# Two of the first group's second-matrix block products computed on two levels in an fp32 Strassen-Winograd kernel on one Trainium2 core

## The chip, the cores and the metric

The kernel runs on one core of one Trainium2 chip. A core has a matrix engine (PE, with its weight loads listed as PEld), a vector engine (DVE), an activation engine (ACT), a general engine (POOL) and a queue engine (SP). Each runs its own instructions strictly in the order in which the program gives them, and waits on semaphores for the others. Transfers are issued by SP, ACT or POOL and carried out by 16 shared DMA engines. The metric is the device time of one execution in microseconds; before the change the median of three runs is 780.52 us (779.9 to 781.32).

## The reference

For 64 batches of 64 channels by 1024 columns, each batch picks one of 16 small matrices; the mixed rows go through a layer of 64 experts of rank 16, of which each token uses its 16 best; the result is added to the input.

```
W   = cond_weights[condition]                    # 64 x (64 x 64)
y   = einsum('bct,bcd->bdt', x, W)               # 4096 tokens x 1024
s   = y @ Wr.T                                   # 64 scores per token
G   = softmax of the 16 largest scores, 0 elsewhere
h   = einsum('nd,krd->nkr', y, A)                # 4096 x (64*16)
out = x + 2 * einsum('nkr,kdr->nd', h * G, B)
```

The kernel multiplies x by A first (product h), mixes the 64 channels of each batch afterwards (the 64x64 matmuls called zp), multiplies by the gates on DVE (into tiles hb), and multiplies by B (product o). So there are two products of 4096 x 1024 by 1024 x 1024 in fp32.

## The kernel before, in words

**Groups and block products.** The 4096 tokens are worked in 8 groups of 512. In each group, h and o are each split into 2 x 2 blocks and computed by seven block products p1 to p7 (the Strassen-Winograd scheme) in place of eight. The operands of p3, p5, p6 and p7 are sums of blocks: on the token side the steps s1 to s4 of `left_sums`, on the matrix side `a_sums` and `b_sums`.

**One level or two.** A block product can be computed directly ("one level", `whole_parent`): for each of two halves of the tokens, 4 matmuls of 128x512, so 8 in all. Or it is split again by the same scheme ("two levels", `parent`): seven leaf products of two matmuls each, 128x256 for o and 128x272 for h. Two levels need four token-side sums per block product on DVE (`prepare`, tiles `l_t`, in the order t1, t2, t3, t4), three copies or adds out of PSUM per ACT and DVE (`copied`, `part`, `third`, `fourth`), and seven matrix-side leaves. Before the change group 0 is computed on one level (its matrices are still arriving and being summed), groups 1 to 7 on two.

**The matrix leaves.** While group 0 runs, DVE makes the leaves of every block of A and B (`leaf_steps`, into tiles of pool `bsum`, five buffers), and POOL stores each to DRAM (`o_p_p` and `h_p_p`, L414). A buffer of `bsum` is free again once its store has landed. Blocks p5, p6, p7 and p4 of B also have three raw quarters stored (`raw_leaves`, L440). From group 1 on, SP fetches leaves back (`fetch`, L461) into a ring of 13 buffers in the order of use; four leaves of h per block stay in SBUF. Five buffers (`bp0`) open when a set of early tiles is given up (`second_level`), eight more (`bp1`) when the whole memory of the first group is (`steady`).

**The order of the work.** Nothing is scheduled by a planner: the program is written out by hand. `run` emits one block product: first half of its matmuls, then what the product before it leaves to do (`done`), then work hung on it as hooks: "mid", the next product's `prepare`, "late", the second half, "end". The tables after L943 say which leaf steps, sums, loads and fetches hang on which product (`h + n` and `o + n` count from the first product of h and of o in group 0). Because every engine works in program order, a step hung early on DVE holds up all that stands behind it.

**Group 0's o.** Before, `FIRST["o"]` is p1, p7, p6, p2, p5, p4, p3. The results are piled up in PSUM banks x, w and y (`PILES`): p6 adds onto p1's bank, p5 onto p6's, p3 onto p5's, p4 onto p7's. At each stage of the pile DVE adds the bank, or a copy of it made by ACT, into one quarter of the output tiles `o`, which POOL loads (L762) and stores (L768).

**The last product.** o's p3 in group 7 has no product after it. Its parts are added straight into the output tiles (`finish`), and two 128-row halves are stored by SP and ACT (L670). Its leaf p4 is accumulated into bank w, which an add of DVE reads first.

Of the kernel before, what the change touches and what calls it, by code (L numbers as in the profile page):

```python
# [29 lines left out]
def kernel(  # L30
# [141 lines left out]
    def scores_t(st):  # L172

        g = st["g"]
        s = acc.tile([P, 2, HN], F32, tag="acc", name=f"st_{g}")
        for h in range(2):
            for c in range(2 * CH):
                e = slice((c % 2) * K, (c % 2 + 1) * K)
                nc.tensor.matmul(
                    s[e, h, :],  # L180
                    lhsT=wr_sb[:, c, :],
                    rhs=xq[g, c // CH, h][:, c % CH, :],
                    start=(h == 0 and c < 2),
                    stop=(c >= 2 * CH - 2),
                    skip_group_check=True,
                )
        st_sb = mp0.tile([P, 2, BANK], F32, tag="m", name=f"st_sb_{g}")[:, 0, :]
        nc.scalar.copy(st_sb, s.rearrange("p h n -> p (h n)"))
        st["st"] = st_sb

    def turn(st):

        g = st["g"]
        sp = acc.tile([P, TPG, K], F32, tag="acc", name=f"sp_{g}")
        for i in range(TPG):
            nc.tensor.matmul(
                sp[:, i, :], lhsT=st["st"][:, ts(i, P)], rhs=two_i, start=True, stop=True
            )
        zr = mp0.tile([P, 2, BANK], F32, tag="m", name=f"zr_{g}")[:, 0, : TPG * K]
        zr = zr.rearrange("p (i k) -> p i k", k=K)  # L200
        nc.scalar.copy(zr, sp)
        st["zr"] = zr
# [137 lines left out]
    def left_sums(l):  # L340
# [35 lines left out]
        "h": ("p1", "p2", "p5", "p6", "p7", "p4", "p3"),  # L376
        "o": ("p1", "p7", "p6", "p2", "p5", "p4", "p3"),
    }
# [12 lines left out]
    for j, (r, c) in {"p1": (0, 0), "p2": (1, 0), "p3": (1, 1)}.items():  # L391
        (q11, _), (q21, q22) = quads(b_t[r, c], HALF)
        leaf_d.update({("o", j, "p1"): q11, ("o", j, "p2"): q21, ("o", j, "p3"): q22})

    unused, to_store = list(hb.values()), []

    def leaf_steps(k, j, block, apart=None):
# [4 lines left out]
        def staged(name):  # L402
            if apart is not None and unused:
                t = unused.pop().rearrange("p c k -> p (c k)")
                return t[:, : 2 * WIDTH[k]].rearrange("p (c k) -> p c k", c=2)
            t = bsum.tile([P, 2 * (HALF + KC)], F32, tag="leaf", name=name)
            return t[:, : 2 * WIDTH[k]].rearrange("p (c k) -> p c k", c=2)
# [34 lines left out]

    parents, to_fetch, ring, stay, fetched = [], [], [], {}, [0]

    def order_of_use():
        for n in range(len(parents) + 1):
            for p in LEAVES:
                m = n - 1 if p in ("p3", "p4") else n
                if 0 <= m < len(parents):
                    par = parents[m]  # L450
                    if par["level"] == 2 and (par["kind"] == "o" or p not in STAY):
                        to_fetch.append((par["kind"], par["j"], p))

    def fetch():
        if to_fetch:
            key = to_fetch.pop(0)
            pool = pools["bp0" if fetched[0] % RING < RING0 else "bp1"]
            fetched[0] += 1
            t = pool.tile([P, 2 * (HALF + KC)], F32, tag="b", name="l{}_{}_{}".format(*key))
            t = t[:, : 2 * WIDTH[key[0]]].rearrange("p (c k) -> p c k", c=2)  # L460
            nc.sync.dma_start(t, leaf_d[key])  # L461
            ring.append((key, t))

    def weights(k, j, p):
        if (k, j, p) in stay:
            return stay[k, j, p]
        key, t = ring.pop(0)
        assert key == (k, j, p)
        return t

# [3 lines left out]
    def parent(kind, st, j, left, done):  # L474

        g = st["g"]
        par = {"kind": kind, "g": g, "j": j, "level": 2, "done": done}

        width = WIDTH[kind]

        def begin():
            name = f"m_{g}_{kind}_{j}"
            if kind == "h" and (g > 1 or j not in ("p1", "p2", "p4")):
                t = pools["zp"].tile([P, 2, 2 * (HALF + KC)], F32, tag="z", name=name)
            else:
                t = pools["mp"].tile([P, 2, 2 * (HALF + KC)], F32, tag="m", name=name)
# [18 lines left out]
        def mm(bank, p, first):  # L505
            w, v = weights(kind, j, p), par["leaf"][p]
            for c in range(2):
# [7 lines left out]
                )  # L515
            if (kind, j, p) not in stay:
                fetch()

        par.update(begin=begin, prepare=prepare, mm=mm)
        return par  # L520

    PILES = {
        "h": dict(p1="X", p2="Y", p5="W", p6="x", p7="x", p4="x", p3="w"),
        "o": dict(p1="X", p7="W", p6="x", p2="Y", p5="x", p4="w", p3="x"),
    }

    def whole_parent(kind, st, j, left, whole, piles, done, copied=None):
# [24 lines left out]
        def copy_out(s):  # L554
            if copied is None:
                return
            if s == 0:
                got["m"] = mp0.tile([P, 2, BANK], F32, tag="m", name=f"m_0_{kind}_{j}")
            nc.scalar.copy(got["m"][:, s, :], piles[n, s])
# [21 lines left out]
    def run(par, before, after, hooks):  # L581
# [34 lines left out]
        if two:  # L616
# [3 lines left out]
            par["copied"] = copied  # L620
            if after is None:
                o = sts[-1]["os"][0, 1][:, 0, :HALF]
                add(o, o, par["bank"]["y"])
                add(o, o, par["val"]["r1"])
            else:
                part(par, 0, 0, "y", "r1")
# [6 lines left out]
        if tail:  # L633
            third()
        if two:
            par["mm"](par["bank"]["x"], "p6", False)
# [9 lines left out]
        if after is None:  # L646
            before["done"](before["m"], before["v"])
            bank("w")
# [10 lines left out]
        for f in hooks["end"]:  # L659
            f()  # L660

    def finish(par, before, st):

        o, q, val = st["os"][0, 1], par["q"], par["val"]

# [3 lines left out]
        def out_tile(s, queue):  # L669
            queue.dma_start(out[ts(st["g"] * TPG + s, P), ts(1, BANK)], o[:, s, :])  # L670

        into(1, 0, val["a"])
        par["mm"](par["bank"]["w"], "p7", True)
        par["mm"](par["bank"]["x"], "p5", False)
        par["copied"]("b")
        into(1, 1, par["bank"]["w"])
        z = acc.tile([P, HALF], F32, tag="acc", name="last_z")
        par["mm"](z, "p3", True)
        par["mm"](par["bank"]["w"], "p4", False)
        into(0, 1, val["b"])  # L680
        into(0, 1, z)
        out_tile(0, nc.sync)
        into(1, 1, val["b"])
        into(1, 0, par["bank"]["w"])
        out_tile(1, nc.scalar)

# [88 lines left out]
    def o_whole(st, whole):  # L775

        piles = {}

        copied = {"p1": (0, 0), "p6": (1, 0), "p5": (1, 1)}
        piled = {"p7": ("w", 1, 1), "p2": ("y", 0, 0), "p4": ("w", 1, 0), "p3": ("x", 0, 1)}  # L780

        def done(j):
            def f(m):
                if j in copied:
                    i, k = copied[j]
                    add(st["os"][i, k], st["os"][i, k], m)
                else:
                    n, i, k = piled[j]
                    add_piled(st["os"][i, k], piles, n)
                if j in ("p2", "p5", "p4", "p3"):  # L790
                    store(st, i, k)

            return f

        return [
            whole_parent("o", st, j, lambda: st["h_ops"], whole, piles, done(j), copied.get(j))
            for j in FIRST["o"]
# [139 lines left out]

    def fetches(n):
        for _ in range(n):
            fetch()  # L940

# [38 lines left out]
    at(o + 1, "mid", gated, st, 0, 1)  # L980
    at(o + 2, "mid", sums, st, "h_sums", "s1")
    at(o + 3, "mid", sums, st, "h_sums", "s4")
    at(o + 3, "end", b_sums, 4)
    for k, lst, n in (
        (h + 2, b_steps, 4),
        (h + 3, b_steps, 2),
        (h + 4, b_steps, 6),
        (h + 5, a_steps, 4),
        (h + 6, a_steps, 5),
        (o, a_steps, 2),  # L990
        (o + 1, b_steps, 7),
        (o + 2, a_steps, 7),
        (o + 3, b_steps, 1),
        (o + 3, a_steps, 2),
        (o + 4, b_steps, 6),
        (o + 5, b_steps, 2),
    ):
        at(k, "end", steps_of, lst, n)
    at(h + 1, "mid", gather, 1)
    for k, (i, j) in enumerate(((0, 0), (1, 0), (0, 1), (1, 1))):  # L1000
        at(o + 1 + k, "mid", load_x, 1, i, j)
    for n, when, j in ((h + 5, "mid", "p5"), (h + 6, "mid", "p6"), (o, "mid", "p7"), (o + 4, "mid", "p4")):
        at(n, when, raw_leaves, j, br[j])
    at(o + 4, "end", second_level)
    at(o + 5, "mid", fetches, 3)
    at(o + 5, "end", fetches, 2)
    h = sts[1]["h"]
    at(h + 0, "mid", fetches, 4)
    at(h + 0, "end", fetches, 4)

# [37 lines left out]
    for st in sts:  # L1048
        g, h, o = st["g"], st["h"], st["o"]
        if not g:  # L1050
            at(h + 6, "mid", load_res, st, (0, 0), (1, 1), (1, 0))
            at(o + 5, "mid", load_res, st, (0, 1))
        else:
# [67 lines left out]
```

## Time and profile before

| What | Value |
|---|---|
| Median of three runs | 780.52 us (779.9 to 781.32) |
| The profiled execution's own time | 780.21 us |
| Its span (first to last event of the core) | 778.4 us |
| DVE busy | 623.8 us (80%) |
| ACT busy | 184.5 us (24%) |
| POOL busy | 73.8 us (9%) |
| Leaf matmul of o, 128x256 | 379 to 383 ns listed, pairs start 0.86 us apart |
| Leaf stores of o by POOL | 28 of 256 KB |

The span is what the core's records cover; the execution's own time has 1.8 us more around it. A line of the timeline gives the start, the duration, the engine, the source line, the operation, its tiles (out<-in, with buffer numbers left out), how often it is repeated, and in square brackets the idle time before it and what ended that. The chain of waits is followed back from the last instruction: each piece is released by the one before it. PE's durations are modelled at their ends, so distances between starts are the better measure of its pace. In the table of stretches the column PEclk is the clock granted to PE, 1.00 being full speed.

### The profile page before, as it was taken

The numbers are of one execution on the slowest core, as the hardware profiler recorded it, in microseconds if no ns is written. First come the engines' busy times: TensorE is split into PE (matmuls) and PEld (weight loads), VectorE is DVE, ScalarE is ACT, GpSimd is POOL, SyncE is SP. The second block draws the span as 40 slices with busy tenths as digits, with TensorE's granted clock in tenths as the row PEclk, the third lists the DMA queues.
The fourth block names the chain that finished last, engine by engine and source line by source line (L and its number), as shares of the span: only waits on it lengthen the run. The fifth ranks groups of instructions, "written<-read, shape, count | busy, mean of one in ns | idle before, by whom it ended". The sixth has DMA issues, their size and how long they took to land.

```text
span 778.4 us, 14669 instructions
## 1 busy us (share of the span) xinstructions
PE 770.6 (99%) x5348; PEld 610.9 (78%) x5348; DVE 623.8 (80%) x1310; ACT 184.5 (24%) x490; POOL 73.8 (9%) x103
## 2 busy tenths in 40 slices
PE   9999999999999999999999999999999999999997
PEld 4445448888888888887888888888888888888886
DVE  4789867678889878897788976889768888688987
ACT  1120002223122222222222222222222231222221
POOL 4235352000200020000200010000200000000000
PEclk9999999999999999999999999999999999999999
DMA  9959678656788768896788958799488893687997
GB/s 331 399 182 332 264 248 300 211 157 238 226 272 298 264 220 287 281 304 226 244 284 278 319 194 283 258 294 330 137 313 268 283 355 113 229 257 250 341 383 259
DMA packets 107607, 208.50 MB, mean 268 GB/s; under 512 B 11072, under 2 KB 27200, under 8 KB 106640
## 3 DMA queue, kind: packets, MB, share of 16 engines
q1 hardware_dynamic: 100496, 186.83, 70.6%
q0 software_dynamic: 6608, 19.95, 7.4%
q8 instruction: 43, 0.70, 0.4%
q10 hardware_dynamic: 432, 0.79, 0.3%
q14 instruction: 28, 0.23, 0.1%
HBM read 174.41 MB, written 33.11 MB: 267 GB/s over the span
## 4 chain that ended last, share of the span: by engine, by line
PE 95%; DVE 3%; DMA 1%; issue 0%; ACT 0%; ACTq 0%; DVEq 0%
PE h_p_x L508 23%; PE o_p_x L508 20%; PE h_p_w L508 12%; PE o_p_w L508 10%; PE h_p_y L508 6%; PE o_p_y L508 5%; PE zp L321 4%; PE o_x L545 4%; PE h_x L545 3%; PE h_w L545 2%; PE o_w L545 2%; DMA x<-in_x_t_dram 1%; DVE o L87 1%; PE sw L221 1%; PE gp L301 1%; PE h_y L545 1%
## 5 line engine op out<-in xcount | busy, mean ns | idle before, releaser
L508 PE MATMUL o_p_x<-lo_p_p,l_t 128*128 128x256 f32 x584 | 142.9, 379 | 0.0
L508 PEld LDWEIGHTS o_p_x<-lo_p_p,l_t 128*128 128x128 f32 x584 | 111.0, 190 | 15.4
L87 DVE TENSOR_TENSOR o<-o,m_o_p 128x1024 f32<-128x1024 f32 x65 | 78.0, 1219 | 0.6
L157 POOL DMA_INDIRECT w_st<-in_cw_dram,idx x32 | 34.9, 1089 | 429.1 <-PE zp L321 412.9
L87 DVE TENSOR_TENSOR m_h_p<-h_p_w,l_a 128x272 f32<-128x272 f32 x49 | 21.6, 440 | 62.6 <-PE h_p_w L508 60.3
L87 DVE TENSOR_TENSOR m_h_p<-m_h_p,m_h_p 128x1088 f32<-128x1088 f32 x49 | 62.3, 1284 | 0.2
L508 PE MATMUL h_p_x<-a,l_t 128*128 128x272 f32 x224 | 60.5, 392 | 0.0
L508 PE MATMUL h_p_w<-lh_p_p,l_t 128*128 128x272 f32 x196 | 53.8, 397 | 0.0
L508 PE MATMUL h_p_x<-lh_p_p,l_t 128*128 128x272 f32 x196 | 52.9, 392 | 0.0
L508 PE MATMUL o_p_w<-lo_p_p,l_t 128*128 128x256 f32 x196 | 51.1, 383 | 0.0
L508 PEld LDWEIGHTS h_p_x<-a,l_t 128*128 128x128 f32 x224 | 42.6, 190 | 8.6
L601 ACT COPY l_b<-h_p_x 128x272 f32<-128x272 f32 x49 | 18.9, 385 | 121.9 <-PE h_p_x L508 117.2
L334 DVE TENSOR_TENSOR hb<-zp,gg 128x512 f32<-128x512 f32 x64 | 39.9, 684 | 7.0 <-PE zp L321 7.0
L508 PE MATMUL h_p_x<-at,l_t 128*128 128x272 f32 x168 | 45.4, 392 | 0.0
L508 PEld LDWEIGHTS h_p_x<-lh_p_p,l_t 128*128 128x128 f32 x196 | 37.2, 190 | 7.5
L601 ACT COPY l_b<-o_p_x 128x256 f32<-128x256 f32 x49 | 18.2, 372 | 103.8 <-PE o_p_x L508 103.8
L508 PEld LDWEIGHTS h_p_w<-lh_p_p,l_t 128*128 128x128 f32 x196 | 36.5, 191 | 7.0
L508 PEld LDWEIGHTS o_p_w<-lo_p_p,l_t 128*128 128x128 f32 x196 | 36.6, 190 | 5.2
L87 DVE TENSOR_TENSOR m_o_p<-o_p_w,l_a 128x256 f32<-128x256 f32 x48 | 20.3, 423 | 22.5 <-PE o_p_w L508 22.5
L321 PEld LDWEIGHTS zp<-w_st,m_h_p 64*64 64x64 f32 x2048 | 31.7, 135 | 7.9 <-issue 7.7
L508 PEld LDWEIGHTS h_p_x<-at,l_t 128*128 128x128 f32 x168 | 31.9, 190 | 6.6
L608 ACT COPY m_h_p<-h_p_x 128x272 f32<-128x272 f32 x49 | 18.9, 385 | 70.7 <-PE h_p_x L508 70.7
(174 smaller groups left out, 1387.3 us busy)
## 6 DMA issues: line engine op xcount, KB each, us to landing
lo_p_p<-o_p_p SPq DMA_DIRECT2D x280, 256.0 KB, 3.7
lh_p_p<-h_p_p SPq DMA_DIRECT2D x147, 272.0 KB, 5.4
lo_p_p<-in_b_t_dram SPq DMA_DIRECT2D x63, 256.0 KB, 4.5
x<-in_x_t_dram SPq DMA_DIRECT2D x31, 512.0 KB, 5.4
o<-in_x_dram SPq DMA_DIRECT2D x28, 512.0 KB, 7.2
out_dram<-o SPq DMA_DIRECT2D x27, 512.0 KB, 5.7
o_p_p<-os_p_p POOLq DMA_DIRECT2D x28, 256.0 KB
b<-in_b_t_dram SPq DMA_DIRECT2D x4, 1024.0 KB, 17.9
```

Source lines behind the costliest of these rows:

```text
L87: nc.vector.tensor_tensor(o, a, b, ALU.add)
L157: nc.gpsimd.indirect_dma_start(out=w_st[:, i, :], out_offset=None, in_=cw, in_offset=bass.IndirectOffsetOnAxis(ap=idx[:, n : n + 1], axis=0),)
L221: nc.tensor.matmul(sw[r, i, ts(k, K // 2)].rearrange("p (d k) -> p d k", d=2), lhsT=ws[g][r, i, :], rhs=halves(st["z"][i // 2, k])[r, i % ...
L301: nc.tensor.transpose(gp[:, i, :], st["g2"][i].rearrange("p a k -> p (a k)"), ident)
L321: nc.tensor.matmul(zp[b][e * D : (e + 1) * D, c, s, :], lhsT=halves(z)[r, s, c // 2, ds(c % 2 * P + e * D, D)], rhs=ws[g][r, 2 * i + s, :] ...
L334: nc.vector.tensor_tensor(tokens(hb[j, i])[:, :, :, b, :], zp[b], g_ij[:, :, :, b, :], ALU.mult)
L508: nc.tensor.matmul(bank, lhsT=v[:, c, :], rhs=w[:, c, :width], start=first and c == 0, stop=c == 1, skip_group_check=True,)
L545: nc.tensor.matmul(piles[n, s], lhsT=left()[j][:, c, ts(s, P)], rhs=w, start=c == 0 and PILES[kind][j].isupper(), stop=c == CH - 1, skip_g ...
L601: nc.scalar.copy(par["val"][n], par["bank"]["x"])
L608: nc.scalar.copy(before["q"][0][1], before["bank"]["x"])
```

## The change

1. In group 0, o's p5 and p3 become two-level products. `FIRST["o"]` becomes p1, p7, p2, p6, p4, p5, p3, so these two are the last before group 1. Their leaves p1 and p2 are used where they lie in SBUF; the other five of each are fetched from DRAM through the ring.
2. p6's value, copied from PSUM, is now added into three quarters of the output one by one, p5's into two, p3's into one.
3. `second_level` and the first five fetches (all of `bp0`) move one product earlier, to o + 3 and o + 4; eight fetches for `bp1` stay at group 1's first product. A used buffer is refilled in its own pool.
4. The six leaves of A's first two blocks are staged in four `hb` tiles, one tile of `mp0` and one of `extra`, none in `bsum`.
5. The hooks of leaf steps, sums s1 and s4, `b_sums(4)` and the raw leaves of p4 move: among others `b_sums(4)` and seven A steps to o + 2, the four p6 steps of B and two A steps to o + 3, two B steps each to o + 5 and o + 6.
6. The last product's leaf p4 gets a bank of its own, p3 is accumulated on bank x, p2's output quarter is added in two halves, and the order of the last adds and stores changes.

```diff
-        "o": ("p1", "p7", "p6", "p2", "p5", "p4", "p3"),
+        "o": ("p1", "p7", "p2", "p6", "p4", "p5", "p3"),
...
+    unused.append(mp0.tile([P, CH, HN], F32, tag="m", name="place_m"))
+    unused.append(extra.tile([P, CH, HN], F32, tag="ex", name="place_ex"))
...
-            if apart is not None and unused:
+            if apart is not None:
...
+        here = STAY if kind == "h" else () if g else ("p1", "p2")
...
+        to_fetch[-2:] = to_fetch[:-3:-1]
+    def fetch(name):
         if to_fetch:
             key = to_fetch.pop(0)
-            pool = pools["bp0" if fetched[0] % RING < RING0 else "bp1"]
-            fetched[0] += 1
-            t = pool.tile([P, 2 * (HALF + KC)], F32, tag="b", name="l{}_{}_{}".format(*key))
+            t = pools[name].tile([P, 2 * (HALF + KC)], F32, tag="b", name="l{}_{}_{}".format(*key))
...
-        "o": dict(p1="X", p7="W", p6="x", p2="Y", p5="x", p4="w", p3="x"),
+        "o": dict(p1="X", p7="W", p2="Y", p6="x", p4="w"),
...
+    def begin_last(par, before, st):
+        o, p = st["os"][0, 0][:, 0, :], st["os"][0, 1][:, 0, :HALF]
+        add(o, o, before["m"][:, 0, :])
+        add(p, p, par["bank"]["y"])
+        add(p, p, par["val"]["r1"])
...
+        mm(w, "p7", True)
+        mm(x_, "p5", False)
+        par["copied"]("b")
+        z = acc.tile([P, HALF], F32, tag="acc", name="last_z")
+        mm(z, "p4", True)
+        mm(x_, "p3", False)
+        q = st["os"][0, 0]
+        add(q[:, 1, :], q[:, 1, :], before["m"][:, 1, :])
+        store(st, 0, 0)
         into(1, 0, val["a"])
-        par["mm"](par["bank"]["w"], "p7", True)
-        par["mm"](par["bank"]["x"], "p5", False)
-        par["copied"]("b")
-        into(1, 1, par["bank"]["w"])
-        z = acc.tile([P, HALF], F32, tag="acc", name="last_z")
-        par["mm"](z, "p3", True)
-        par["mm"](par["bank"]["w"], "p4", False)
...
+        into(1, 1, w)
+        into(1, 0, w)
+        into(1, 1, val["b"])
+        into(1, 0, z)
+        out_tile(1, nc.scalar)
+        into(0, 1, x_)
         out_tile(0, nc.sync)
...
+                elif j == "p6":
+                    kept["a"] = m
+                    into(1, 0, m)
+                    into(1, 1, m)
+                elif j == "p4":
+                    into(1, 0, pile="w", last=True)
+                    into(0, 1, kept["a"])
+                elif j == "p5":
+                    into(1, 1, m, last=True)
+                    into(0, 1, m)
...
-    at(o + 2, "mid", sums, st, "h_sums", "s1")
-    at(o + 3, "mid", sums, st, "h_sums", "s4")
-    at(o + 3, "end", b_sums, 4)
+    at(o + 3, "mid", sums, st, "h_sums", "s1")
+    at(o + 4, "mid", sums, st, "h_sums", "s4")
+    at(o + 2, "end", b_sums, 4)
...
-        (h + 3, b_steps, 2),
-        (h + 4, b_steps, 6),
+        (h + 3, b_steps, 4),
+        (h + 4, b_steps, 4),
...
-        (o + 1, b_steps, 7),
+        (o + 1, b_steps, 8),
         (o + 2, a_steps, 7),
-        (o + 3, b_steps, 1),
+        (o + 3, b_steps, 4),
         (o + 3, a_steps, 2),
-        (o + 4, b_steps, 6),
         (o + 5, b_steps, 2),
+        (o + 6, b_steps, 2),
...
-    at(o + 4, "end", second_level)
-    at(o + 5, "mid", fetches, 3)
-    at(o + 5, "end", fetches, 2)
+    at(o + 3, "end", second_level)
+    at(o + 4, "mid", fetches, RING0, "bp0")
```

## The prediction

> **What bounds the kernel now.** I read the page's busy shares and chain first, then the chain piece by piece, then the timeline of DVE and POOL while group 0's o runs, and last the end of the span.
>
> ```profile
> PE 770.6 (99%) x5348; PEld 610.9 (78%) x5348; DVE 623.8 (80%) x1310; ACT 184.5 (24%) x490; POOL 73.8 (9%) x103
> PE 95%; DVE 3%; DMA 1%; issue 0%; ACT 0%; ACTq 0%; DVEq 0%
> ```
>
> PE sets the time: 95% of the chain, and hardly 8 us of the span without a matmul. So a matmul saved is worth its whole duration, and a wait of PE costs its whole length, wherever it lies. The chain, group 0:
>
> ```profile
> 54.94 0.68 DVE m_h_p L87
> 55.62 0.04 issue
> 55.66 7.13 PE h_w L545 x16
> ...
> 80.40 6.87 PE o_x L545 x16
> 87.26 6.87 PE o_y L545 x16
> ...
> 114.73 0.92 PE h_p_x L508 x4
> ```
>
> Only one DVE piece stands here (0.72 us at 54.94); a one-level product takes 6.87 us, and PE then runs without a gap into group 1. Now DVE and POOL in the same stretch:
>
> ```profile
> 96.22 2.29 DVE L90 TENSOR_TENSOR b<-b,bt 128x2048 f32<-128x2048 f32 x1
> 98.42 0.68 DVE L90 TENSOR_TENSOR os_p_p<-b 128x512 f32<-128x512 f32 x1
> 99.02 0.72 DVE L90 TENSOR_TENSOR hs_p_p<-a 128x544 f32<-128x544 f32 x1
> 99.77 0.72 DVE L90 TENSOR_TENSOR hs_p_p<-a,hs_p_p 128x544 f32<-128x544 f32 x1
> 100.42 1.28 DVE L87 TENSOR_TENSOR o<-o,o_y 128x512 f32<-128x512 f32 x2
> 101.61 0.69 DVE L90 TENSOR_TENSOR os_p_p<-bt 128x512 f32<-128x512 f32 x1
> 101.99 0.71 POOL L768 DMA_DIRECT2D out_dram<-o  x1 [0.65 <-DVE o L87]
> 102.70 2.13 POOL L440 DMA_DIRECT2D o_p_p<-b  x3
> 104.44 3.05 POOL L414 DMA_DIRECT2D o_p_p<-os_p_p  x5
> 108.83 0.69 DVE L90 TENSOR_TENSOR os_p_p<-b,os_p_p 128x512 f32<-128x512 f32 x1 [3.88 <-DMA o_p_p<-os_p_p]
> 112.98 0.42 DVE L87 TENSOR_TENSOR l_t<-x 128x256 f32<-128x256 f32 x1
> 113.43 0.42 DVE L90 TENSOR_TENSOR l_t<-l_t,x 128x256 f32<-128x256 f32 x1
> ```
>
> Two things are to be seen. DVE adds bank y at 100.42, though PE finished it at 94.13: it runs six us behind PE. And it stands 3.88 us for a buffer whose leaf was made at 101.61 but whose store POOL could issue only at 104.44, behind an output store and three raw leaves. Both are free now, because one-level products need little from DVE; the first that PE needs is t2 of group 1 (ended 113.85, used near 116.5).
>
> **The change, part by part.** *Matmuls.* One level is 8 matmuls, 6.87 us. Two levels are seven leaves of 0.864 (o leaves run as 1.73 for two in the chain), 6.05 us. Two products: 2 x 0.82 = 1.64 us less on PE.
>
> *Staging.* All five `bsum` buffers are now free when the B steps begin at 31.99. In the profile the fourth step waited 5.60 us, until 39.73, for a store; now the sixth is the first to wait, for the same store. DVE does the score routing, six B steps in place of four, and `b_sums(1)` with this lead; the add before PE's h_w, at 54.93, comes at about 51.6. PE is ready at 54.94, so the 0.72 us piece goes: -0.7 us. The other moved hooks up to here are covered: PE's next needs (hb with s3, ended 71.92 for a use at 71.97 before) come earlier too. If the lead were lost, 0.7 us would stay.
>
> *The DVE queue ahead of p5.* This decides. Let E be the end of PE's p2, now third of the seven and two products ahead of p5: 80.40 + 6.87 - 0.72 = 86.5. `b_sums(4)` overwrites the matrix that p2 reads, so DVE cannot start it before E; by then it has the rest of its queue done (its wait at 81 to 84.6 for leaf stores shrinks, because stores are issued some 2 us earlier and five fetches of SP that landed around 78 to 84 have moved away; before, it would be through near 87.8, 1.3 after E). From E, in program order, with distances between starts in the trace:
>
> - `b_sums(4)` 2.20 (96.22 to 98.42); seven A steps 4.95 (the same seven ran 88.99 to 93.94); two adds of y 1.19; s1 1.13 (a 1024 add); four B steps 2.66 (101.61 to 104.27); one A step 0.75: E + 12.88.
> - the second A step, which needs a `bsum` buffer; the sixth one back is the first of those four B steps, so it waits for that store.
> - then 0.65, two adds of p6's copy, s4 (3 x 1.14), t1 0.45, t2 0.42: 4.94.
>
> PE meanwhile: p6 and p4 (2 x 6.87), then p5's leaves p1 and p2 (1.73), which read a tile made at s1: E + 15.47. The next leaf needs t2. Without a wait for the store DVE has t2 at E + 17.82: PE stands 2.35 us. The store: POOL must issue the output store when the y adds end (E + 8.34 + 0.29), then the three raw leaves, then this one, exactly the sequence shown above, where 6.84 us lie between the output store's issue (101.99) and DVE's release (108.83). There the queue was already 1.6 us behind with older stores, here by my sum about 1.0, so 6.2: release at E + 14.9, t2 at E + 19.8, **PE stands 4.4 us**. With the full 6.84 it is 4.9, and with DVE 1.3 late at E 6.2; below, 2.35. I take 4.4: the copied sequence is the nearest row. Behind the waiting A step stand all output adds, s4 and `prepare`; only PE waits for those.
>
> *After that.* DVE has t3, t4, one part, the w adds (1.19), one 1024 add, t1 and t2 of p3: about 4.3 us; PE has six leaves, 5.2. The 1024 add needs the fourth output tile, loaded by POOL after the late A step's store; about 1 us of slack. Each of `bp0`'s five buffers is refilled on use and needed 5.2 us later; o fetches in group 1 land in 3.7 us at the median, those of h in 5.4, and here POOL's stores run beside them. 0 to 1.5 us, I take 0 (o fetches are the nearer row). Group 1's first fetches wait on group 0's last output store, as before, with five us in hand.
>
> *Extra DVE and ACT work* of the two products (8 token sums of 0.42, 6 parts, 3 more 1024 adds) is inside the sums above; ACT's copies are hidden, it is 24% busy.
>
> *The clock.* [...]
>
> ```profile
> 773.60 1.13 PE L508 MATMUL o_p_w<-lo_p_p,sum_p 128*128 128x256 f32 x4 [0.93 <-DVE o L87]
> ...
> 774.77 0.42 DVE L87 TENSOR_TENSOR o<-o,o_p_w 128x256 f32<-128x256 f32 x1
> ```
> ```profile
> 776.00:776.20 0.20, 0.00 (x0) 0.00 (x0) 0.00 (x0) 0.00 (x0) 0.00 (x0) 1.00 0.56 205
> 776.20:776.40 0.20, 0.00 (x0) 0.00 (x0) 0.00 (x0) 0.00 (x0) 0.00 (x0) 0.58 1.02 389
> 776.40:776.60 0.20, 0.00 (x0) 0.00 (x0) 0.00 (x0) 0.00 (x0) 0.00 (x0) 0.50 1.02 389
> ```
>
> The row: the clock fell to half at 776.23, 1.5 us after the last matmul. [...] I take 1.5; no run here shows a gap of this length inside the work.
>
> *The end.* Leaf p4 no longer waits 0.93 us for DVE, so DVE bounds: after the add that ended at 770.17 come two adds of 512 (about 0.6 each), ten of 256 (0.34, with 0.1 to 0.2 more where one needs the last), against one 1024 and nine of 256 ending at 775.19 before. I get 774.8: -0.4 us (0 to -0.8).
>
> Sum: -1.64 - 0.7 - 0.4 + 4.4 + 1.5 = +3.1 us on the profiled 780.21, whose span is 778.4. That execution lies 0.3 below the median; I add to the median: **783.6 us**.
>
> **The rivals.** *The stall without the clock:* the same gap, full clock: 780.52 + 1.6 = 782.1, with the short stall 780.1. [...] *No stall, the other side:* if DVE reached t2 by E + 15.47, only the gains stay: 780.52 - 2.74 = 777.8. It needs 2.35 us less DVE work between `b_sums(4)` and t2 and no store wait; the gain passes into loss where the stall exceeds 2.7 us. Against it: each duration is a measured one of the same instruction, and DVE cannot pass its own queue.
>
> **How the numbers follow.** Stall with clock 0.47 (782.3 to 785.5), stall alone 0.21 (780.1 to 783.2), more late 0.18 (785 to 789), no stall 0.14 (777.3 to 779). Range 779.8 to 787.0: it leaves out nearly all of the last and a third of the third case, 2 in 10. About 0.2% is what a measurement can tell from no change: 779.0 to 782.1. Faster is the last case less a little, 0.13; within, half of the stall alone and some of its neighbours, 0.17; slower 0.70.
>
> **What would show it.** Right: a gap of 2 to 5 us on PE before the third leaf of group 0's o p5, its releaser an l_t subtraction of DVE; ahead of that DVE idle some 2 us before an A step, for a leaf store; the granted clock at half somewhere in the next 7 us; no 0.7 us gap before h_w; no 0.93 us wait in the last leaves; 24 more PE pieces (each fp32 matmul is listed as two, and two products go from 8 to 14). Wrong: PE going through p5 without a gap, because DVE was further ahead; or a gap elsewhere, at fetched leaves of p3 or group 1; or full clock after the gap.

## The result

The changed kernel takes 786.79 us at the median (785.49 to 787.75), the kernel before 780.62 us (779.9 to 781.53) beside it: a ratio of 1.0076, 95% interval 1.0063 to 1.0089. It is slower by 6.2 us. The prediction was 783.6 us: the right sign, half the loss, and a time inside the range, but only 0.2 us below its upper end of 787.0; two of the six executions lay above it. All later comparisons with the kernel before stand against its runs on the chips of the experiments, 780.83 to 780.84 us at the median.

### The profile page after: what moved, and what is told of

Same layout as the page of the kernel before. It is cut to its first block, busy times and chain, and to the rows that moved or that the text cites. A ratio compares the mean times of both kernels' runs of the same rounds, so it can differ in the third digit from the quotient of the medians.

```text
span 785.7 us, 14781 instructions
## 1 busy us (share of the span) xinstructions
PE 772.1 (98%) x5372; PEld 618.6 (79%) x5372; DVE 632.3 (80%) x1327; ACT 186.8 (24%) x496; POOL 74.7 (10%) x103
## 4 chain that ended last, share of the span: by engine, by line
PE 95%; DVE 2%; issue 1%; ACT 0%; POOL 0%; DVEq 0%; POOLq 0%
PE h_p_x L517 23%; PE o_p_x L517 21%; PE h_p_w L517 12%; PE o_p_w L517 11%; PE h_p_y L517 6%; PE o_p_y L517 5%; PE zp L322 4%; PE h_x L558 4%; PE o_w L558 2%; PE h_w L558 2%; PE o_x L558 2%; PE sw L222 1%; DVE o L87 1%; PE gp L302 1%; PE o_y L558 1%
## 5 line engine op out<-in xcount | busy, mean ns | idle before, releaser
L517 PE MATMUL o_p_x<-lo_p_p,l_t 128*128 128x256 f32 x612 | 151.8, 383 | 5.0 <-issue 5.0
L517 PEld LDWEIGHTS o_p_x<-lo_p_p,l_t 128*128 128x128 f32 x612 | 117.3, 192 | 21.9 <-issue 5.4
L87 DVE TENSOR_TENSOR o<-o,m_o_p 128x1024 f32<-128x1024 f32 (+1 forms) x70 | 82.8, 1203 | 0.5
L517 PE MATMUL o_p_w<-lo_p_p,l_t 128*128 128x256 f32 x204 | 54.1, 388 | 0.0
L517 PEld LDWEIGHTS o_p_w<-lo_p_p,l_t 128*128 128x128 f32 x204 | 38.7, 193 | 5.6
```

The source lines that it names most:

```text
L87: nc.vector.tensor_tensor(o, a, b, ALU.add)
L517: nc.tensor.matmul(bank, lhsT=v[:, c, :], rhs=w[:, c, :width], start=first and c == 0, stop=c == 1, skip_group_check=True,)
```

## The profile after

The profiled execution took 787.5 us, with a span of 785.7. Two rows of its page:

```profile
PE 772.1 (98%) x5372; PEld 618.6 (79%) x5372; DVE 632.3 (80%) x1327; ACT 186.8 (24%) x496; POOL 74.7 (10%) x103
PEclk9999989999999999999999999999999999999999
```

There are 24 PE pieces more, as worked out, and one slice of 40, the sixth (98 to 118 us), in which the granted clock is not full. The chain of waits through that stretch (start, duration, what):

```profile
51.62 3.63 PE h_x L558 x8
55.25 6.87 PE h_w L558 x16
...
79.72 6.87 PE o_y L558 x16
86.59 6.87 PE o_x L558 x16
...
101.19 0.86 PE o_p_y L517 x4
102.05 5.04 issue
107.08 2.05 PE o_p_x L517 x4
...
110.84 2.94 PE o_p_x L517 x8
...
118.96 0.92 PE h_p_x L517 x4
```

Three things are to be seen. The DVE piece ahead of h_w is gone. PE stands 5.04 us before the third leaf of group 0's o p5 (the chain calls it "issue", since the subtraction for t2, which the leaf reads, had ended 0.1 us before). And the leaves behind the gap are slow: the ten from 107.08 to 118.96 take 11.88 us where ten take 8.65 at full clock. DVE and POOL in the timeline of the same execution:

```profile
86.63 2.29 DVE L90 TENSOR_TENSOR b<-b,bt 128x2048 f32<-128x2048 f32 x1 [1.31 <-PE o_y L558]
...
95.35 0.72 POOL L789 DMA_DIRECT2D out_dram<-o  x1 [1.41 <-DVE o L87]
96.06 2.13 POOL L444 DMA_DIRECT2D o_p_p<-b  x3
...
97.80 2.53 POOL L418 DMA_DIRECT2D o_p_p<-os_p_p  x4
...
102.06 0.73 DVE L90 TENSOR_TENSOR hs_p_p<-a,hs_p_p 128x544 f32<-128x544 f32 x1 [2.57 <-DMA o_p_p<-os_p_p]
...
106.56 0.42 DVE L90 TENSOR_TENSOR l_t<-l_t,sum_p 128x256 f32<-128x256 f32 x1
```

This is the queue of the prediction, instruction by instruction. E, the end of PE's p2, is 86.59, and DVE had stood 1.31 us for it. The output store is issued at 95.35, three raw leaves behind it, then the leaf store that the second A step waits for; DVE is released at 102.06, 6.71 us after the output store's issue, and t2 ends at 106.98. The table of stretches shows the clock (columns: stretch, its length; busy time and count of PE, PEld, DVE, ACT, POOL; PEclk; DMA share; GB/s):

```profile
106.40:109.40 3.00, 2.31 (x6) 1.90 (x7) 2.97 (x8) 0.23 (x1) 0.00 (x0) 0.50 0.31 123
109.40:112.40 3.00, 3.00 (x9) 2.38 (x8) 2.35 (x5) 0.14 (x1) 0.73 (x1) 0.50 0.71 257
...
113.20:114.00 0.80, 0.80 (x5) 0.72 (x4) 0.80 (x2) 0.18 (x1) 0.00 (x0) 1.00 0.59 207
```

In the trace's record of the clock it is at half from 106.35 for 6.827 us, twice 3.413.

**The account.** I take the start of the same PE piece, counted from the end of the program, in both traces. At group 1's start PE is 5.96 us later than before: -0.68 when group 0's third o product begins (80.40 before, 79.72 after; PE ran 0.32 late from its start on, and the staging brought 1.0), -1.64 for the two products, +5.04 of gap, +3.23 of slow leaves. Of the span's 7.3 us the rest is +1.13 near 205 us, -0.67 between 300 and 400 and +1.22 at 741 (short stops of PE, below), and -0.36 at the end. The medians differ by 6.17; the changed kernel's profiled execution lies 0.7 above its median, that of the kernel before 0.3 below.

## The experiments

| Run | Median us | Ratio to before (95%) | PE's gap at p5's third leaf |
|---|---|---|---|
| changed kernel | 786.79 | 1.0076 (1.0063 to 1.0089) | 5.04 |
| e3_warm | 783.13 | 1.0032 (1.002 to 1.0044) | 0.58, ahead of it dummy work |
| e4_raw_later | 782.85 | 1.0029 (1.0018 to 1.004) | 2.51 |
| e2_one_step | 781.65 | 1.0008 (1.0002 to 1.0015) | 1.73 |
| e1_no_gap | 779.68 | 0.9985 (0.9979 to 0.9992) | none |
| e8_bp1_later | 779.86 | 0.9992 (0.9985 to 0.9998) | none |
| e7_shift | 779.63 | 0.9987 (0.998 to 0.9995) | none |
| e9_one_more_stays | 779.14 | 0.9977 (0.9967 to 0.9986) | none |
| e10_stays_shift | 778.24 | 0.9963 (0.995 to 0.9977) | none |
| e5_staging (from before) | 779.47 | 0.9983 (0.9977 to 0.999) | no such leaf |
| e6_tail (from before) | 781.17 | 1.0002 (0.9994 to 1.001) | no such leaf |

The first theory: all of the loss is DVE's queue between the end of p2 and t2, and what the clock makes of the gap. Its rivals: the loss lies in the fetched leaves, in the DMA engines, or in the other parts of the change.

### No gap

```diff
-        (o + 2, a_steps, 7),
-        (o + 3, b_steps, 4),
+        (o + 2, a_steps, 3),
+        (o + 3, b_steps, 2),
...
-        (o + 5, b_steps, 2),
-        (o + 6, b_steps, 2),
+        (o + 5, b_steps, 3),
+        (o + 6, b_steps, 3),
...
+    at(o, "mid", steps_of, a_steps, 2)
+    at(o + 2, "mid", steps_of, a_steps, 2)
```

> The changed kernel with hooks alone moved: of the seven A steps behind b_sums(4) at o + 2 four go earlier (two at o 'mid', two at o + 2 'mid'), and of the four B steps at o + 3 two go later (three each at o + 5 and o + 6). Theory (the loss is DVE's queue between the end of p2 and t2, and what the clock makes of it): from the end E of PE's p2, DVE needs 2.2 (b_sums) + 3 x 0.71 (A steps) + 1.2 (y adds) + 1.1 (s1) + 2.7 (four steps in the two hooks) + 4.4 (adds, s4, t1, t2) = 13.6 us, and PE asks for t2 at E + 15.5: no gap of PE before the third leaf of p5, full clock afterwards, and only the gains stay: 780.6 - 1.64 - 0.7 - 0.4 = 777.9 us (777.3 to 778.9), ratio to before 0.9965. Rival (what the changed kernel lost lies elsewhere too, in late fetches of p3 and of group 1 or in PE's later short stops): the gap goes but 780 to 783 us are left. Second rival (the steps moved earlier only move the wait forward, since the store queue of POOL is what is full): DVE waits for a buffer at o or at o + 2 'mid' and PE's gap stays at 2 us or more, 782 to 785 us.

Measured: 779.68 us. The chain of this kernel:

```profile
100.74 0.86 PE o_p_y L517 x4
101.60 0.86 PE o_p_x L517 x4
102.47 0.86 PE o_p_w L517 x4
...
108.54 5.98 DMA lo_p_p<-o_p_p
114.52 0.14 issue
114.66 1.10 PE o_p_w L517 x4
```

The gap is gone, the granted clock is 1.00 in every stretch from 96 to 122 us (its mean is 0.998 or more in all 21 executions), and the time falls by 7.1 us: DVE's queue and the clock did make the loss. Six hook lines, with all the rest of the change in place, turn it from 0.8% slower into 0.15% faster than before. The second rival falls. But 1.8 us of the expected gain are missing, and the first rival has a share in them: the last leaf of p3, issued by SP at 108.54 when its ring buffer came free, landed 5.98 us later, and PE waited 0.97 us more than between two leaves. In the changed kernel the same leaf had the same lead (issued at 117.27 for a use at 122.41) and was in time. Another 0.33 us lie outside the span: this kernel, like the four built on it (e7 to e10), has 2.1 us there, all others 1.8; why was not found. The rest are in the main short stops of PE, taken up below.

### One step

```diff
-        (o + 3, a_steps, 2),
+        (o + 3, a_steps, 1),
+        (o + 4, a_steps, 1),
```

> The changed kernel with one step moved: the second of the two A steps at o + 3, the one that waited 2.57 us for a bsum buffer, goes to o + 4, behind prepare of p5. Theory (the gap of 5.0 us is 2.6 of that wait and 2.4 of DVE's own work): DVE reaches t2 3.3 us earlier (2.57 wait and 0.73 step), the gap of PE is 1.7 us (1.3 to 2.2), too short for the clock to fall: 786.8 - 3.3 - 3.2 = 780.3 us (779.5 to 781). [...] Second rival (the loss is the amount of DVE work, the wait only filled time that would have been lost anyway): the gap stays above 3.5 us, 784 to 786.5.

Measured: 781.65 us, above the expected 780.3. The chain:

```profile
102.19 1.73 issue
103.93 1.10 PE o_p_x L517 x4
```

The gap is 1.73 us as expected: moving one step of 0.73 us took 3.31 us away, 2.57 of them the wait for its buffer. So the rival that takes the wait for mere filling falls. The clock stayed full, 1.00 from 102 to 110 us in the trace (in all 21 executions its mean is 0.998 or more). Of the missing 1.3 us, 0.67 lie a little later (PE waits for an ACT copy and a leaf of p3). The rest isn't placed: PE's short stops are no longer here than in the changed kernel's trace, but that trace's execution itself lies 0.7 us above its median.

### Raw leaves later

```diff
-    for n, when, j in ((h + 5, "mid", "p5"), (h + 6, "mid", "p6"), (o, "mid", "p7"), (o + 3, "mid", "p4")):
+    for n, when, j in ((h + 5, "mid", "p5"), (h + 6, "mid", "p6"), (o, "mid", "p7"), (o + 4, "mid", "p4")):
```

> The changed kernel with the three raw leaves of p4 stored one product later (o + 4 'mid' for o + 3 'mid'), so that in POOL's queue the four B-step stores stand right behind the output store. All DVE steps stay. Theory (the buffer comes free late because the raw leaves stand ahead of the leaf store in POOL's queue): DVE's wait of 2.57 us falls to 0 to 1, t2 comes 1.6 to 2.6 us earlier, the gap of PE is 2.4 to 3.4 us: 784.2 to 785.2 us if the clock still falls for as long, 781 to 782 if it stays full at such a gap. Rival (the buffer is late because the stores share the DMA engines, not for the order of issue): the wait stays above 2 us, 786 to 787 us.

Measured: 782.85 us. The timeline, where DVE no longer waits, and the stretches:

```profile
97.00 0.57 POOL L418 DMA_DIRECT2D o_p_p<-os_p_p  x1 [1.02 <-DVE os_p_p L90]
...
98.68 0.72 DVE L90 TENSOR_TENSOR hs_p_p<-a 128x544 f32<-128x544 f32 x1
99.44 0.73 DVE L90 TENSOR_TENSOR hs_p_p<-a,hs_p_p 128x544 f32<-128x544 f32 x1
```
```profile
104.00:105.30 1.30, 0.83 (x4) 0.78 (x5) 1.30 (x5) 0.00 (x0) 0.00 (x0) 1.00 0.56 183
105.40:108.70 3.30, 3.30 (x9) 2.62 (x8) 2.84 (x5) 0.37 (x1) 0.72 (x1) 0.50 1.04 401
108.80:110.00 1.20, 1.20 (x7) 1.05 (x6) 1.20 (x5) 0.49 (x2) 0.00 (x0) 1.00 0.98 338
```

The three 256 KB stores ahead of it in POOL's queue made the leaf's store late. With them moved behind, it is issued at 97.00, only 0.80 us earlier than in the changed kernel, but it has landed by 99.44, so within 2.44 us, where it took 4.26 (97.80 to 102.06), and the A step runs without a wait. Whether they delay it by their place in the queue or by their load on the DMA engines isn't parted: the engines' share from 97.0 to 99.5 is 0.84 here and 0.96 in the changed kernel. The gap is now DVE's own work alone, 2.51 us (the prediction's lower bound was 2.35). And the clock falls here too, but for half as long (1.00 up to 105.3, 0.50 from 105.4 to 108.7, 1.00 from 108.8 on), and by the means not in each execution: of the seven, three have a mean granted clock of 0.997 and took 783.5 to 783.8 us, four have 0.998 to 0.999 and took 782.4 to 782.9. That is why the median lies between the two values expected. Only the first of the seven has a trace, so that the gap was 2.51 us in the other six too is assumed.

### Work in the gap

```diff
+        if two and par["g"] == 0 and par["j"] == "p5":
+            warm = acc.tile([P, P], F32, tag="acc", name="warm")
+            for _ in range(20):
+                nc.tensor.matmul(warm, lhsT=ident, rhs=ident, start=True, stop=True)
```

> The changed kernel with 20 matmuls of 128x128 by 128x128 added on PE, results unused, in a spare PSUM bank, between p5's leaves p2 and p6, where PE stood for 5.0 us. By the leaf's row (128x256, fp32: 0.43 us) 20 of half the size fill about 4.3 us, so PE's gap is 0.7 us, while t2 comes at the same time. Nothing else changes. Theory (a stall of 5.0 us and, apart from it, 3.2 us for two clock windows at half speed): the clock stays full, 786.8 - 3.2 = 783.6 us (783 to 784.3). Rival (the ten leaves after the gap were slow for a cause of their own: late tiles from DVE or late fetches, that the shown clock only goes along with): 786 to 787.5. If the extra matmuls take longer than the gap, the excess is added: at 0.3 us each 6 us, + 1.0.

Measured: 783.13 us. The chain:

```profile
101.99 4.46 PE warm L645 x40
106.46 0.58 issue
107.04 1.10 PE o_p_x L517 x4
```

The third leaf starts at 107.04, in the changed kernel at 107.08: DVE is no earlier, PE merely isn't idle. From there to group 1's first leaf PE takes 8.87 us (107.04 to 115.91), in the changed kernel 11.88. The granted clock is 1.00 from 102 to 112 us. So the clock alone costs 3.0 us, and the rival that looks for a cause of its own in the slow leaves falls. Behind it PE slips 0.58 us within group 1's first product (0.2 of them a wait for an add of DVE), as it doesn't in the changed kernel, and two short stops (1.23 and 1.17) are missing and one (0.63) is new: together -4.1 us in the spans, -3.7 in the medians.

### Staging alone and the end alone

Staging, put into the kernel before:

```diff
+    unused.append(mp0.tile([P, 2, BANK], F32, tag="m", name="place_m"))
+    unused.append(extra.tile([P, CH, HN], F32, tag="ex", name="place_ex"))
...
-            if apart is not None and unused:
+            if apart is not None:
```

> The kernel before with the staging part alone: the six first leaves of A in tiles of hb, mp0 and extra, none in bsum. Theory (as in the prediction): the wait for a store before the fourth B step ends or comes later, DVE is about 3.3 us earlier, and the 0.72 us piece of DVE before PE's h_w goes: 780.8 - 0.7 = 780.1 us (779.5 to 780.5), ratio 0.9991. Rival (the early DVE steps only meet the next late store, so that the add is still late): 780.5 to 781.2 and the piece is still in the chain.

Measured: 779.47 us, 1.4 below before, and more than expected. Its chain:

```profile
51.44 3.63 PE h_x L547 x8
55.07 6.87 PE h_w L547 x16
61.93 2.15 PE o_x L547 x5
```

The DVE piece is gone, and h_w takes 6.87 us where it took 7.13 behind the wait. From a start 0.14 us later PE is 0.86 earlier at o's first product: 1.0 us from the trace, not 0.7. The changed kernel's trace and the first experiment's give the same 1.0 over this stretch. The median says 1.4, with an interval of 0.8 to 1.8. So this part is worth somewhat more than forecast.

The end, put into the kernel before, in its core:

```diff
+        mm(z, "p4", True)
+        mm(x_, "p3", False)
...
+        into(1, 0, z)
+        out_tile(1, nc.scalar)
+        into(0, 1, x_)
         out_tile(0, nc.sync)
```

> The kernel before with the end alone: the last product's leaf p4 in a bank of its own, p3 on bank x, the last adds and stores in the new order. Theory: the 0.93 us wait of PE for DVE goes, DVE then bounds, and the end comes 0.4 us earlier: 780.8 - 0.4 = 780.4 us (780.0 to 780.7), ratio 0.9995. Rival (the stores bound the end, whatever DVE does): no change, 780.8, with the wait gone all the same.

Measured: 781.17 us; no difference to before that could be told. The last rows of the timeline before, then of this kernel:

```profile
774.43 0.34 SPq L670 DMA_DIRECT2D out_dram<-o  x1
775.22 0.35 ACTq L670 DMA_DIRECT2D out_dram<-o  x1
```
```profile
774.82 0.41 DVE L87 TENSOR_TENSOR o<-o,o_p_x 128x256 f32<-128x256 f32 x1
774.93 0.35 ACTq L676 DMA_DIRECT2D out_dram<-o  x1
775.26 0.34 SPq L676 DMA_DIRECT2D out_dram<-o  x1
```

PE's wait of 0.93 us is gone and, counted from the same PE piece, DVE's last add starts 0.35 us earlier. But the two last stores are now issued 0.33 us apart, where it was 0.79, and the last packet ends 2.28 us after the later issue, where it was 1.71. So 0.35 us gained on DVE became 0.22 lost from that piece to the last packet; in the changed kernel's own trace 0.24 us are gained. The rival is nearer: what DVE gains here the stores take back, in part or wholly.

### The late leaf of p3

Two kernels on top of the first one. The fetches behind it one step later:

```diff
-    at(h + 0, "mid", fetches, 4, "bp1")
-    at(h + 0, "end", fetches, RING - RING0 - 4, "bp1")
+    at(h + 0, "end", fetches, 4, "bp1")
+    at(h + 1, "mid", fetches, RING - RING0 - 4, "bp1")
```

> The first experiment's kernel with the eight fetches for bp1 one step later each (four at group 1's first product 'end', four at its second 'mid'). In its trace PE waited 0.97 us for the last leaf of group 0's p3, issued by SP at 108.54 and landed at 114.52, with five fetches of 272 KB issued right behind it from 109.40 on. Theory (these five share the DMA engines with it): it lands in 4 to 5 us and PE's wait falls to 0 to 0.2: 779.7 - 0.9 = 778.8 us (778.4 to 779.3). Rival (the stores of POOL, or simply its late issue, make it late): the wait stays near 0.9, 779.4 to 780; and if the delayed fetches are needed sooner than they land, a new wait in group 1, 780 to 781.5.

Measured: 779.86 us, no gain. From the list of PE's waits:

```profile
PE o_p_w L517 <- DMA lo_p_p<-o_p_p: 1.2, 1, 1.2
```

The theory isn't tested by it: the edit moved too little. The four fetches issued while the leaf was under way start at 109.43, 110.29, 112.99 and 113.93, in the first experiment at 109.40, 110.27, 112.96 and 113.88; only the fifth starts later (116.22 for 115.79), when the leaf has landed in both. One fetched leaf less:

```diff
+        if (kind, j, g) == ("o", "p5", 0):
+            here = ("p1", "p2", "p3")
...
-            (q11, _), (q21, _) = quads(whole[j], HALF)
-            stay.update({("o", j, "p1"): q11, ("o", j, "p2"): q21})
+            (q11, _), (q21, q22) = quads(whole[j], HALF)
+            stay.update({("o", j, "p1"): q11, ("o", j, "p2"): q21, ("o", j, "p3"): q22})
```

> The first experiment's kernel (no gap) with one fetched leaf less: leaf p3 of group 0's o p5 is used where it lies in SBUF too, as its p1 and p2 are, so that four leaves of p5 and five of p3 go through the ring and the last leaf of p3 is fetched at the use before (near 107.7 for 108.54). Theory (the wait of 0.97 us near 113.7 is that fetch, late because a ring of five buffers lets it start only then, and 6.0 us on the full DMA engines are not to be shortened by moving others): the wait is 0 to 0.2, 779.7 - 0.85 = 778.8 us (778.3 to 779.3). Rival (the DMA engines are full and the leaf lands at the same time whenever it is issued): the wait stays, 779.5 to 780.

Measured: 779.14 us, and in the profiled execution no wait. But my reasoning was wrong: the leaf is still issued at 108.69, since a fetch is triggered by a use, and I had taken away one of each. It landed in under 5.2 us here; in the last kernel below, with the same fetches, in 6.35, and PE waited 1.17 us. So this leaf's lateness varies from trace to trace between 0 and 1.2 us, at DMA shares of 0.9 to 1.1 around it. The share doesn't order the cases: from the leaf's issue on over 5.15 us it is 1.00 in the first experiment, 0.99 here without a wait, and 0.93 in the kernel that waited 1.17. That the full DMA engines set it stays a guess; how much of the 0.5 us to the first experiment's median comes from the one leaf less stays open. Single executions can be worse: one of 21 of the kernel with the later fetches took 783.31 us and one of 14 of the next section's first kernel 782.25, both at a mean granted clock of 0.997; neither has a trace, so why is open.

### The short stops

```diff
-    for _ in range(10):
-        nc.tensor.matmul(idle, lhsT=ident, rhs=ident, start=True, stop=True)
+    for _ in range(17):
+        nc.tensor.matmul(
+            idle[:32, :32], lhsT=ident[:, :32], rhs=ident[:, :32], start=True, stop=True
+        )
+    for _ in range(5):
+        nc.tensor.matmul(idle, lhsT=ident, rhs=ident, start=True, stop=True)
```

> The first experiment's kernel (no gap before p5's third leaf) with the ten matmuls at the very start, which do nothing but keep PE busy until x has landed at 5.4 us, replaced by 17 small ones (32x32) and five of the old: 12 matmuls more, that is 24 pieces and 24 weight loads, and the start of h_x should stay where x lands. All that PE does later is the same, 48 instructions further on in its stream. In the first experiment's trace PE stood 1.24 us at 196.3 and about 0.5 us at 733, both right after a 16 KB transfer of the queue named instruction (195.2 and 730.6), with nothing awaited that the profile shows. [...] Rival (the stop belongs to the work there, a bank or a tile that is late): it stays at 1.2 us in the same place of the program and the time at 779.7, plus up to 0.5 if the small matmuls delay the start.

Measured: 779.63 us, no gain in the median, which is the rival's number; what the traces say of the stops follows. The same on top of the kernel with one more leaf in SBUF, with 29 small matmuls and one of the old:

```diff
-    for _ in range(10):
-        nc.tensor.matmul(idle, lhsT=ident, rhs=ident, start=True, stop=True)
+    for _ in range(29):
+        nc.tensor.matmul(
+            idle[:32, :32], lhsT=ident[:, :32], rhs=ident[:, :32], start=True, stop=True
+        )
+    nc.tensor.matmul(idle, lhsT=ident, rhs=ident, start=True, stop=True)
```

> The same, with the ten matmuls at the very start replaced by 29 small ones and one of the old, so that all of PE's later instructions stand 80 further on in its stream (as they did behind the 20 extra matmuls in the third experiment, which had no stop near 200 and only 0.4 us in a zp stage). Theory (stops by late instructions depend on where a zp stage falls between two 16 KB transfers): no stop of PE near group 1's end, one of about 0.6 us near 270 instead: 0.6 to 1.2 us below the other kernel of this call, 777.6 to 778.3, if the start is not late. Rival (a shift only moves the stops, and their sum over the execution stays): no difference to the other kernel of over 0.3 us in the medians.

Measured: 778.24 us, 0.9 below the kernel with one more leaf in SBUF, in spite of the late leaf. PE in the timelines of three kernels; first the changed one, near group 1's end and in a zp stage of group 7:

```profile
202.08 2.09 PE L322 MATMUL zp<-w_st,m_h_p 64*64 64x64 f32 x128
205.34 0.85 PE L517 MATMUL h_p_w<-lh_p_p,l_t 128*128 128x272 f32 x3 [1.17 <-issue]
```
```profile
737.96 1.98 PE L322 MATMUL zp<-w_st,m_h_p 64*64 64x64 f32 x120
740.93 0.34 PE L322 MATMUL zp<-w_st,m_h_p 64*64 64x64 f32 x8 [0.99 <-issue]
```

Shifted by 48 instructions, no stop at the first place, and in the same zp stage of group 7 one further forward:

```profile
194.31 2.10 PE L326 MATMUL zp<-w_st,m_h_p 64*64 64x64 f32 x128
...
196.34 1.18 PE L521 MATMUL h_p_w<-lh_p_p,l_t 128*128 128x272 f32 x4
```
```profile
729.31 1.63 PE L326 MATMUL zp<-w_st,m_h_p 64*64 64x64 f32 x96
731.95 0.69 PE L326 MATMUL zp<-w_st,m_h_p 64*64 64x64 f32 x32 [1.01 <-issue]
```

Shifted by 80, near group 1's end:

```profile
194.85 2.10 PE L325 MATMUL zp<-w_st,m_h_p 64*64 64x64 f32 x128
196.87 1.18 PE L522 MATMUL h_p_w<-lh_p_p,l_t 128*128 128x272 f32 x4
```

The stop moves with the instruction stream and not with the work. In group 7's stage it comes after piece 120 in the changed kernel and in the five others without a shift of PE's stream, and after piece 96 in the shifted one: 24 pieces with their 24 weight loads are the 48 instructions of the shift. The two kernels shifted by 80, this one and the one with work in the gap, have no stop at either place and one of 0.42 us near 270, after the same piece; that was forecast from the one for the other. The page lists a queue named instruction with 43 packets of 16 KB. In the changed kernel's trace such a packet starts 2.50 us before PE goes on at 205.34 and 2.33 before it goes on at 740.93. In the twelve traces there are 16 unexplained stops inside groups 1 to 7 that leave more than 0.6 us between the starts of two PE pieces; in each, such a packet starts 2.3 to 2.6 us before PE goes on. Whether PE stands there for instructions that the packet brings was not shown. By number PE's 10,744 pieces and weight loads are some 250 for each of the 43 packets, and a zp stage's 128 pieces and 128 weight loads run in 2.1 us, less than the 2.3 to 2.6 from the packet's start. Which stops appear changed with the instructions ahead: behind the late leaf, one shift brought 0.5 us in the trace (it also delayed the start by 0.3), the other 1.5. The 48 instructions that the change adds are such a shift.

The kernel with both, 778.24 us, beats the one before (0.9963) and the changed one.

## Why the prediction was half right

**Two products, -1.64.** Right: the first experiment stands 1.72 us ahead of before at group 1's start: -1.12 by the staging and a start 0.12 us earlier (79.28 for 80.40), -1.64, +0.97 for the late leaf make -1.79.

**Staging, -0.7.** Right in kind, undersized: 1.0 us in three traces, because h_w behind the wait had also taken 7.13 us for 6.87.

**The stall, 4.4.** Right in its mechanism, its place and its pieces; measured 5.04. The output store was issued at E + 8.76 (I had E + 8.63), and the release came 6.71 us later, where I had shortened the copied 6.84 to 6.2 because POOL's queue would be less far behind. That correction was wrong: the whole copied sequence held, and 4.9 had been written beside it. The wait was 2.57 us, DVE's work the other 2.5; two experiments took either apart.

**The clock, 1.5.** The term that failed in size: 3.0 us. No run shows the 1.5, which was my estimate: the row at the end of the kernel before shows that the clock fell, after 3.41 us with 1.13 us of PE work (772.82 to 776.23), but not for how long. In the runs it was at half for 6.83 us after the gap of 5.04 us, at a price of 3.0, and for 3.4 us after the gap of 2.51, at a price of 1.7 (10.56 us from the third leaf to group 1's first, for 8.87 at full clock). That it would fall was right: all six executions have a mean clock of 0.995 to 0.996, where the kernel before has 0.998 or more beside the experiments. In the traced one the 3.41 us before the fall, 102.94 to 106.35, held no PE work at all; in the kernel with the raw leaves later the 3.4 us up to 105.3 held 0.9 us (26%). The first half of the 6.83 us, 106.35 to 109.76, held PE's remaining idle time, 0.73 us, and PE ran 2.68 of 3.41 us, 79%; the clock stayed at half through the second half, which was full of work. With the raw leaves later the half-speed stretch was full of work (3.30 of 3.30 us from 105.4 to 108.7), and there the clock came back after it. The price is half of 6.83 less that idle time, 3.05.

**The fetched leaves, 0.** Right for the changed kernel. In the five kernels without a gap the last leaf of p3, with the same lead of about 5.15 us, cost 0 to 1.2 us; why is open, so this term was right in part by luck.

**The end, -0.4.** DVE was earlier as worked out, but I ended the sum at DVE's last add; the two stores behind it, issued closer together, take a part back, and alone the edit shows no gain.

**What no step held.** The short stops: +1.7 us in the profiled execution (1.13 - 0.67 + 1.22), about 0.6 in the medians by what is left of 6.17 after 5.96 and -0.36. The list of PE's waits before shows one of 0.4 us, which I passed over.

**The sum.** I forecast +3.1 and measured +6.2. The missing 3 us are 1.5 to 1.7 of clock, 0.6 of stall and about 0.6 of short stops; the staging's surplus of 0.3 was lost in that trace by a later start. The time lay inside the range by 0.2 us, in a part of it held for the case "more late", of which only the longer time at half clock came; that is luck.

**The rivals.** The case "more late" (785 to 789) holds the time and was held at 0.18. What came of it is the 6.83 us at half clock; DVE was early at E, by the 1.31 us that it stood there, and no fetch was late. "The stall without the clock" is what the work in the gap shows; "no stall" is the first experiment.

## What to carry to other kernels

When PE sets the time and a second engine must prepare its operands, work out that engine's queue in program order from the last event that can hold it, with every buffer wait in it and with all that stands ahead in the store queue that frees the buffer; here one 0.73 us step, one place earlier than it need be, cost 3.3 us of stall and the clock on top. A PE gap is priced with its clock, here 3.0 us beside a gap of 5.04. In these traces the clock fell after 3.4 us with 0, 0.9 and 1.13 us of PE work, a half-speed stretch of 3.41 us that was 79% busy didn't bring it back, and a full one did; a half-speed stretch of 3.4 us full of work cost 1.7 us. If the gap can't be closed, filling it with idle matmuls gives that part back (3.0 us here). Before a change of a few tenths of a percent is judged, look for PE stops that end 2.3 to 2.6 us behind the start of an instruction queue's packet: 48 and 80 instructions more moved them here.

## What was unexpected in the hardware

- The clock fell after 3.4 us that held 0.9 us of PE work (26%). At this gap of 2.51 us the mean clock is 0.997 in three of seven executions and 0.998 or 0.999 in four; at a gap of 1.73 us it is 0.998 or more in all 21. 3.41 us that were 79% busy did not restore it.
- PE stops of 0.4 to 1.2 us behind 16 KB packets of the queue named instruction, at zp stages, where 128 pieces and 128 weight loads run in 2.1 us; they come and go as the number of PE instructions ahead changes, and 48 more moved one by just 48.
- The same 256 KB fetch, issued at the same point, took from under 5.2 to 6.4 us in five kernels that differ little.
- The first experiment's kernel and those built on it have 2.1 us outside the span, all others 1.8; the cause is open.
